# A two-layer convolution and attention kernel: pairing of products, column halves in attention, and other PSUM banks

## The chip, the cores and the metric

The kernel runs on one core of a Trainium2 chip. The metric is the device time of one execution in microseconds. Each engine (PE, the matrix engine; DVE, the vector engine; ACT, the scalar engine; POOL; and SP, which here only issues DMAs) works through its own queue in order, and they wait for one another by semaphores.

## The reference

The input is an image x of 384 channels and 192 × 192 pixels, float32. Two layers are applied, each as x + layer(group norm of x), with 32 groups of 12 channels:

```
layer 0:  qkv = W_qkv · x + b            # 384 -> 1152 channels per pixel
          qkv = 2x2 max pool of qkv      # 96 x 96 pixels
          qkv = depthwise 3x3 conv of qkv + b_dw
          q, k, v: 8 heads of 48 channels; q and k normed over the 9216 pixels
          attn = q · kᵀ * temperature    # 48 x 48 per head, over the pixels
          out = sum over 4 values of kk of  a_kk * softmax(top kk of attn) · v
          out = gelu(out), each pixel repeated 2x2, W_proj · out + b_proj
layer 1:  sign(x), shifted along the row by -3..3 by channel, times sign(W) (384 x 384), + bias
```

The attention weights per head are 48 × 48, so that layer 0 is mostly products over pixels: the qkv projection in float32 is by far the largest.

## The kernel before

The image is cut into 24 units (`NU`) of 8 rows; 384 channels are 3 tiles (`CT`) of 128 partitions. The stages are:

1. Statistics of x for the first group norm, while x streams through (ends at about 140 us).
2. q and k, for each of the 24 units and for m = 0 to 5 (3 tiles of q, 3 of k): `qkv_unit` makes three blocks of 512 pixels with 3 products each (L354) into the PSUM ring `qkv` of 3 banks; DVE takes the 2 × 2 maximum from PSUM (L364); ACT adds the bias (L373) and makes the first of the nine taps of the depthwise convolution (L380); DVE adds the other eight (L382); ACT keeps the last two rows for the next unit (L384). Below, a *tile* of work is such a run of `qkv_unit` for one unit and one m. A product in float32 appears in the profile as two matmul records with two weight loads; so a tile is 18 records of 512 columns. The result is transposed in 32 × 32 blocks (L410) and moved by 16 SP DMAs for each of q and k (L423, L428) into `room`, an SBUF buffer that holds one unit of q and k. `products` (L433 to L449) multiplies q and k of one unit into three PSUM banks `gram`, by halves of 64 columns (6 products for each 128 pixels); it is called for unit u − 1 after tile m = 2 of unit u (L465), and its instructions are pinned in program order. `gathered` (L470) does the last unit.
3. v, 24 units of 3 tiles, by the same `qkv_unit`, into `chunk` buffers in SBUF. In the first units the softmax steps (`softmaxes`, a generator, one step per tile) lie between the tiles. At its end it transposes the 384 × 384 weight matrix `full` into `aT` in 9 pieces, each a PE transpose into the one bank `p3ps` (L576) and an ACT copy (L577). After that, `attention(g)` (L626) treats 512 pixels: the array is used as four row tiles of 32 partitions, one for each pair of heads (p = 0 to 3); each multiplies its 32 rows of three channel tiles t, which are 96 channels of two heads, into 96 output columns and its own bank `ops`. Six GELUs on ACT (L644) take a block from PSUM back into `chunk`. There are 18 blocks (`NAB`); 16 are done between tiles of v, and two (`HOLD`) after the last tile, in an order written by hand.
4. Projection (L589, then the addition by DVE, L601) and layer 1: ACT takes the signs (L782), POOL shifts them, PE multiplies in fp8 (L801) into three double banks `l1ps`, DVE adds (L810), and DMAs store. For i = 0 to 3 the projections are ahead of the first layer-1 products; the projections use two banks `yps`.

Where nothing is pinned, a scheduler puts each engine's instructions in order; `manual_schedule` and `keep_in_program_order` fix the order as written. `pool.tile(name=...)` takes the next buffer of a ring of `bufs` and so waits for the users of the buffer that stood there.

How the channels of a head pair lie in a row tile matters for the change (`pair_rows`, L109): t = 0 holds 32 channels of the first head, t = 1 holds 32 of the second, and t = 2 holds the remaining 16 of each.

Of the kernel before, what the change touches and what calls it, by code (L numbers as in the profile page):

```python
# [10 lines left out]
F32 = mybir.dt.float32  # L11
# [4 lines left out]
AF = mybir.ActivationFunctionType  # L16
# [4 lines left out]
P = 128  # L21
# [128 lines left out]
def conv_preact_kernel(ctx: ExitStack, tc: tile.TileContext, a: dict, out: bass.AP):  # L150
# [192 lines left out]

        return (1 if u else 2), (PR if u < NU - 1 else PR + 1)

    def qkv_unit(pqkv, xt, u, m, pl, parts, before=None):


        x4 = xt.rearrange("p t (r w) -> p t r w", w=W)
        lo, hi = rows(u)  # L350
        for r0, nr, c0, ncol in BLOCKS:
            ps = pqkv.tile([P, 512], F32, name="qkv")
            for t in range(CT):
                ins = nc.tensor.matmul(  # L354
                    ps,
                    wq[:, t, m * P : (m + 1) * P],
                    x4[:, t, r0 : r0 + nr, c0 : c0 + ncol],
                    start=(t == 0),
                    stop=(t == CT - 1),
                )  # L360
                if m == CT and t == r0 == c0 == 0:

                    tc.keep_in_program_order(ins)
            nc.vector.tensor_reduce(  # L364
                pl[:, 2 + r0 // 2 : 2 + (r0 + nr) // 2, 1 + c0 // 2 : 1 + (c0 + ncol) // 2],
                ps.rearrange("p (i a j b) -> p i j a b", a=2, b=2, j=ncol // 2),
                AX.XY,
                ALU.max,
            )
        if before:  # L370
            before(pqkv.tile([P, 512], F32, name="qkv")[:, :NM])
        new = pl[:, 2 : 2 + PR, 1 : 1 + WP]
        nc.scalar.activation(new, new, AF.Identity, bias=bq[:, m : m + 1])  # L373
        for acc, r0, n in parts:
            acc2 = acc.rearrange("p (r w) -> p r w", w=WP)
            for k in range(9):
                r = lo - 1 + r0 + k // 3
                src = pl[:, r : r + n, k % 3 : k % 3 + WP]
                if k == 0:
                    nc.scalar.activation(acc2, src, AF.Identity, bias=bdw[:, m : m + 1], scale=wdw[:, m, 0:1])  # L380
                else:
                    nc.vector.scalar_tensor_tensor(acc2, src, wdw[:, m, k : k + 1], acc2, ALU.mult, ALU.add)  # L382
        if u < NU - 1:
            nc.scalar.copy(pl[:, 0:2, :], pl[:, PR : PR + 2, :])  # L384


    last_products = products_of_x.enter_context(ExitStack())
    pg = last_products.enter_context(tc.tile_pool(name="p2g", bufs=1, space=PSUM))
    with pairs, tc.tile_pool(name="p2t", bufs=2, side="right") as tp:
        gram = [pg.tile([P, 512], F32, name=f"gram{t}") for t in range(CT)]  # L390
        qkT = room[:, : 2 * size].rearrange("p (s n) -> p s n", s=2)

        def of_unit(u):

            lo, hi = rows(u)
            n = hi - lo + 1
            nk = -(-n * WP // P)
            q, k = qkT[:, 0, : nk * C], qkT[:, 1, : nk * C]
            return (
                n,  # L400
                nk,
                q.rearrange("p (t k c) -> p t k c", t=CT, k=nk),
                k.rearrange("p (b k c) -> p b k c", k=nk, c=B),
            )
# [46 lines left out]
        for u in range(NU):  # L451

            for v in range(u, u + KEEP + 1):
                if v not in kept:
                    kept[v] = unit(v % NU)
            xt = kept.pop(u)
            lo, hi = rows(u)
            n = hi - lo + 1
            for m in range(2 * CT):
                acc = tp.tile([P, (PR + 1) * WP], F32, name="dw")[:, : n * WP]  # L460
                qkv_unit(pqkv, xt, u, m, padded_qk[m], [(acc, 0, n)], None if u or m else bias)
                transposed(u, *divmod(m, CT), acc)
                sq = tp.tile([P, (PR + 1) * WP], BF16, name="sq", bufs=1)
                nc.scalar.activation(sq[:, : n * WP], acc, AF.Square, accum_out=ssq[:, m, u : u + 1])  # L464
                if u and m == CT - 1:  # L465
                    products(u - 1)
                if m % CT == CT - 1:
                    moved(u, m // CT)

# [8 lines left out]

    wpr = ctx.enter_context(tc.tile_pool(name="wpr", bufs=1)).tile([P, CT, C], F32, name="wpr")

    def softmaxes(p3, psp):


        ones = p3.tile([P, P], F32, name="ones")
# [78 lines left out]
        for t in range(CT):  # L563
            for j in range(DN[t] // HD):
                pair, second = divmod(HEAD0[t] + j, 2)
                for d, e0, e1 in (
# [3 lines left out]
                    nc.vector.tensor_scalar_mul(  # L570
                        full[:, t, d : d + e1 - e0], wsum[:, t, e0:e1], headm[:, t, j : j + 1]
                    )
        for t in range(CT):
            for k in range(CT):
                ps = psp.tile([P, P], F32, name="p3ps")
                nc.tensor.transpose(ps, full[:, t, k * P : (k + 1) * P], ident)  # L576
                nc.scalar.copy(aT[:, k, t * P : (t + 1) * P], ps)  # L577


    end = ctx.enter_context(ExitStack())  # L580
# [29 lines left out]
    with ExitStack() as vs:  # L610
# [5 lines left out]
        pool = first_pooled  # L616
        for t in pool:
            nc.gpsimd.memset(t[:, 0:2, :], 0.0)  # L618
        done, steps = 0, None

        def weights(name):
            wl = wp.tile([P, CT, C], F32, name="wl")
# [2 lines left out]

        def attention(g):  # L626

            c, b = divmod(g, CPX // ABLK)
            cols = slice(b * ABLK, (b + 1) * ABLK)
            pss = [po.tile([P, ABLK], F32, name="ops") for _ in range(NP)]  # L630
            for t in range(CT):
                for p in range(NP):
                    rows = slice(p * Q, (p + 1) * Q)
                    nc.tensor.matmul(  # L634
                        pss[p][:PAIR],
                        aT[rows, t, p * PAIR : (p + 1) * PAIR],
                        chunk[c][rows, t, cols],
                        start=(t == 0),
                        stop=(t == CT - 1),
                    )  # L640
            for p, ps in enumerate(pss):
                for t in [p] if p < CT else range(CT):
                    src, to = (slice(0, PAIR),) * 2 if p < CT else (slice(t * Q, (t + 1) * Q), slice(PAIR, P))
                    nc.scalar.activation(chunk[c][to, t, cols], ps[src], AF.Gelu, accum_out=osum[to, t, g : g + 1])  # L644

        for u in range(NU):
            xt = kept.pop(NU + u) if NU + u in kept else unit(u)
# [8 lines left out]
            for m in range(CT):  # L656
                parts = []
                for c in range(first // CR, last // CR + 1):
# [1 line left out]
                    parts.append(  # L660
                        (chunk[c][:, m, (r0 - c * CR) * WP : (r1 + 1 - c * CR) * WP], r0 - first, r1 + 1 - r0)
                    )
                qkv_unit(pqkv, xt, u, 2 * CT + m, pool[m], parts)
                if m == 0 and u == UC:

                    wl = weights("w_projG").rearrange("p t (g c) -> p t g c", c=GRP)
# [12 lines left out]
                    group_sums(bg, bpr.unsqueeze(2))  # L679
                    nc.vector.tensor_scalar_mul(bg1, bg, -1.0 / GRP)  # L680
                if u >= TOPK and steps is None:
                    steps = softmaxes(p3, psp)
                if steps:
                    if next(steps, 1):
                        steps = ()
                        scratch.close()
                        early = opened("p5x0", 1)
                elif steps == () and done < NAB - HOLD and (done + 1) * ABLK <= first * WP:
                    attention(done)
                    done += 1  # L690
        kept[FIRST[1] - 1] = unit(FIRST[1] - 1)
        with tc.manual_schedule():

            assert done == NAB - HOLD
            for g in range(done, NAB - 1):
                attention(g)
            for m in range(CT):
                projected(pqkv.tile([P, 512], F32, name="qkv")[:, :PPX], FIRST[0], m)
            attention(NAB - 1)

            projected(pqkv.tile([P, 512], F32, name="qkv")[:, :PPX], FIRST[1], 0)
            nc.vector.tensor_reduce(om, osum, AX.X, ALU.add)
            ys = [pqkv.tile([P, 512], F32, name="qkv")[:, :PPX] for m in range(1, CT)]
            projection(ys[0], FIRST[1], 1)
            projection(ys[1], FIRST[1], 2, range(1))
            ps = psp.tile([P, P], F32, name="p3ps")[:NG, :1]
            for t in range(CT):
                nc.tensor.matmul(ps, wg1[:, t], om[:, t : t + 1], start=(t == 0), stop=(t == CT - 1))
            nc.vector.tensor_scalar(gm, ps, -1.0 / (GRP * NPX), bg1, ALU.mult, ALU.add)
            projection(ys[1], FIRST[1], 2, range(1, 2))  # L710
            ps = psp.tile([P, P], F32, name="p3ps")[:, :CT].unsqueeze(2)
            spread(ps, gm)
            projection(ys[1], FIRST[1], 2, range(2, CT))
            added(ys[0], FIRST[1], 1, 0)
            nc.vector.tensor_add(nmean1, nmean0, ps[:, :, 0])
            added(ys[0], FIRST[1], 1, 1)
            for r in range(2):
                added(ys[1], FIRST[1], 2, r)
# [4 lines left out]
    with end:  # L723
# [18 lines left out]
        def summed(i, m):  # L742

            u = order[i]
            if i >= len(FIRST):
                projected(pyp.tile([P, PPX], F32, name="yps"), u, m)
            if m < CT - 1:
                return
            left[u // UC] -= 1
# [43 lines left out]
        def finished(i, m):  # L793
# [3 lines left out]
            for r0 in range(0, UR, 4):  # L797
                ps = psp.tile([P, 2, 512], F32, name="l1ps")
                for j in range(2):
                    for t in range(CT):  # L800
# [4 lines left out]
                            start=(t == 0),  # L805
                            stop=(t == CT - 1),
                        )
                px = slice(r0 * W, (r0 + 4) * W)
                blk = xt[:, m, px].rearrange("p (j n) -> p j n", j=2)
                nc.vector.scalar_tensor_tensor(  # L810
                    blk, ps[:, :, : 2 * W], bl1[:, m : m + 1], blk, ALU.add, ALU.add
                )
                if (i, m) == (NU - 1, CT - 1):
                    nc.sync.dma_start(ov[u, :, m, px], xt[:, m, px])
            if i + 3 >= NU and (i, m) != (NU - 1, CT - 1):
                nc.sync.dma_start(ov[u, :, m], xt[:, m])

# [104 lines left out]
```

## Time and profile before

Three timed runs took 2224.49, 2224.65 and 2229.05 us (median 2224.65). The profiled execution has a span of 2225.2 us at a granted TensorE clock of 0.998; its own time was 2227.01 us.

| engine | busy us | share of the span |
|---|---|---|
| PE | 2072.8 | 93% |
| DVE | 1902.6 | 85% |
| ACT | 819.6 | 37% |
| POOL | 211.3 | 9% |

| group | count | busy us | mean ns |
|---|---|---|---|
| L354 qkv matmul | 3888 | 1681.4 | 593 |
| L441 gram matmul (96 and 128 columns) | 876 | 90.7 | 248, 277 |
| L634 attention matmul | 432 | 52.0 | 601 |
| L644 GELU, 32 and 96 partitions | 108 | 63.1 | 587 |
| L382 depthwise taps, q and k | 1152 | 708.6 | 615 |
| L364 maximum | 648 | 441.5 | 682 |

Busy times of matmuls overlap one another since they are pipelined; what a run of them costs is read from the distance of their starts. In the chain of waits each line names the instruction that held up what came after it, with the time that it so accounts for; in the timeline the bracket at the end of a line is the idle time of the engine before it and what ended that.

### The profile page before, as it was taken

The numbers are of one execution on the slowest core, as the hardware profiler recorded it, in microseconds if no ns is written. First come the engines' busy times: TensorE is split into PE (matmuls) and PEld (weight loads), VectorE is DVE, ScalarE is ACT, GpSimd is POOL, SyncE is SP. The second block draws the span as 40 slices with busy tenths as digits, with TensorE's granted clock in tenths as the row PEclk, the third lists the DMA queues.
The fourth block names the chain that finished last, engine by engine and source line by source line (L and its number), as shares of the span: only waits on it lengthen the run. The fifth ranks groups of instructions, "written<-read, shape, count | busy, mean of one in ns | idle before, by whom it ended". The sixth has DMA issues, their size and how long they took to land.

```text
span 2225.2 us, 20427 instructions
## 1 busy us (share of the span) xinstructions
PE 2072.8 (93%) x6573; PEld 966.5 (43%) x6573; DVE 1902.6 (85%) x3270; ACT 819.6 (37%) x1419; POOL 211.3 (9%) x330
## 2 busy tenths in 40 slices
PE   0049999999999999999999999999999999999998
PEld 0024444444444444444444444443444444455555
DVE  5678888888888888888888899986787887899998
ACT  4542222222222222222222222225323233388886
POOL 1000000000000000000000000000000000177765
PEclk9999999999999999999999999999999999999999
DMA  9962222222222232222223213014221312379997
GB/s 398 417 280 64 64 69 71 84 87 72 67 64 71 68 103 71 72 64 66 72 70 101 70 33 121 28 49 175 85 85 45 125 43 86 128 295 407 424 425 319
DMA packets 209723, 302.73 MB, mean 136 GB/s; under 512 B 162224, under 2 KB 165072, under 8 KB 209616
## 3 DMA queue, kind: packets, MB, share of 16 engines
q1 hardware_dynamic: 199296, 248.18, 32.1%
q10 hardware_dynamic: 10320, 53.25, 5.8%
q8 instruction: 52, 0.85, 0.1%
q14 instruction: 55, 0.45, 0.1%
HBM read 216.04 MB, written 56.62 MB: 123 GB/s over the span
## 4 chain that ended last, share of the span: by engine, by line
PE 81%; DVE 11%; DMA 5%; ACT 1%; SPq 1%; issue 0%; DVEq 0%; ACTq 0%
PE qkv L354 64%; PE l1ps L801 6%; PE yps L589 6%; DVE chunk L382 5%; DMA xt<-in_x_dram 5%; DVE pooled L364 2%; PE gram L441 2%; PE ops L634 2%; DVE dw L382 1%; SPq L186 1%; DVE xt L601 1%; ACT chunk L380 0%; ACT pooled L373 0%; PE qkv L273 0%; SPq L428 0%
## 5 line engine op out<-in xcount | busy, mean ns | idle before, releaser
L354 PE MATMUL qkv<-xt,wq 128*128 128x512 f32 x3888 | 1681.4, 593 | 0.0
L354 PEld LDWEIGHTS qkv<-xt,wq 128*128 128x128 f32 x3888 | 734.4, 190 | 920.8 <-issue 837.1
L382 DVE SCALAR_TENSOR_TENSOR dw<-pooled,small,dw 128x384 f32<-128x384 f32 (+2 forms) x1152 | 708.6, 615 | 132.3 <-ACT dw L380 107.7
L364 DVE TENSOR_REDUCE pooled<-qkv 128x128 f32<-128x512 f32 x648 | 441.5, 682 | 37.9 <-PE qkv L354 37.3
L382 DVE SCALAR_TENSOR_TENSOR chunk<-pooled,small,chunk 128x384 f32<-128x384 f32 (+3 forms) x696 | 369.6, 545 | 71.4 <-ACT chunk L380 54.1
L384 ACT COPY pooled<-pooled 128x196 f32<-128x196 f32 x207 | 73.6, 356 | 756.6 <-DVE dw L382 536.8
L373 ACT ACTIVATE pooled<-pooled,small 128x384 f32<-128x384 f32 x216 | 133.0, 616 | 384.0 <-DVE pooled L364 373.5
L782 ACT ACTIVATE signs<-xt,nmean 64x1536 fp8e4<-64x1536 f32 x144 | 226.5, 1573 | 44.7 <-PE yps L589 26.0
L801 PE MATMUL l1ps<-signs,wb 128*128 128x384 fp8e4 x864 | 152.2, 326 | 0.0
L589 PE MATMUL yps<-chunk,wpr 128*128 128x384 f32 x396 | 141.2, 495 | 2.7 <-DVE xt L601 2.7
L601 DVE SCALAR_TENSOR_TENSOR xt<-yps,small,xt 128x768 f32<-128x768 f32 x132 | 128.1, 1012 | 13.8 <-PE yps L589 7.3
L273 PE MATMUL qkv<-wq,late 128*32 128x384 f32 x18 | 8.3, 622 | 140.3 <-ACT late L295 140.3
L810 DVE SCALAR_TENSOR_TENSOR xt<-l1ps,small,xt 128x768 f32<-128x768 f32 x144 | 138.3, 1007 | 0.0
L301 DVE BATCH_NORM_STATS2 room<-xt 128x6 f32<-128x512 f32 x144 | 88.1, 678 | 51.0 <-DMA xt<-in_x_dram 50.9
L618 POOL MEMSET pooled<- 128x196 f32 x3 | 0.8, 263 | 1285.6 <-DVE dw L382 1285.6
L464 ACT ACTIVATE sq<-dw 128x384 bf16<-128x384 f32 (+2 forms) x144 | 75.3, 523 | 120.7 <-DVE dw L382 120.6
L801 PEld LDWEIGHTS <-wb 128*128 128x128 fp8e4 x864 | 83.7, 97 | 72.3 <-issue 14.2
L380 ACT ACTIVATE dw<-pooled,small 128x384 f32<-128x384 f32 (+2 forms) x144 | 100.5, 698 | 2.2
L290 ACT ACTIVATE room<-xt 128x1536 bf16<-128x1536 f32 x48 | 71.2, 1483 | 66.4 <-DMA xt<-in_x_dram 65.7
L589 PEld LDWEIGHTS yps<-chunk,wpr 128*128 128x128 f32 x396 | 74.7, 193 | 45.8 <-issue 5.9
L410 DVE STREAM_TRANSPOSE blocks<-dw 128x384 f32<-128x384 f32 (+1 forms) x144 | 82.2, 571 | 4.2
L760 POOL COPY rest<-signs 9x384 int32<-9x384 int32 (+1 forms) x144 | 72.4, 503 | 67.3 <-ACT signs L782 61.9
(116 smaller groups left out, 576.9 us busy)
## 6 DMA issues: line engine op xcount, KB each, us to landing
xt<-in_x_dram SPq DMA_DIRECT2D x81, 2304.0 KB, 13.6
out_dram<-xt ACTq DMA_DIRECT2D x17, 2304.0 KB, 15.6
room<-blocks SPq DMA_DIRECT2D x736, 36.0 KB, 2.0
xt<-in_x_dram SPq DMA_DIRECT2D x26, 768.0 KB, 8.8
out_dram<-xt ACTq DMA_DIRECT2D x12, 768.0 KB, 8.6
out_dram<-xt SPq DMA_DIRECT2D x8, 768.0 KB, 4.8
wq<-in_w_qkvT_dram ACTq DMA_DIRECT2D x1, 1728.0 KB, 15.2
room<-blocks SPq DMA_DIRECT2D x32, 48.0 KB, 2.0
```

The costliest lines, as they stand in the source:

```text
L301: nc.vector.bn_stats(stats[b][:, t, at : at + 6], xt[:, t, j * 512 : (j + 1) * 512])
L354: ins = nc.tensor.matmul(ps, wq[:, t, m * P : (m + 1) * P], x4[:, t, r0 : r0 + nr, c0 : c0 + ncol], start=(t == 0), stop=(t == CT - 1),)
L364: nc.vector.tensor_reduce(pl[:, 2 + r0 // 2 : 2 + (r0 + nr) // 2, 1 + c0 // 2 : 1 + (c0 + ncol) // 2], ps.rearrange("p (i a j b) -> p i j ...
L373: nc.scalar.activation(new, new, AF.Identity, bias=bq[:, m : m + 1])
L380: nc.scalar.activation(acc2, src, AF.Identity, bias=bdw[:, m : m + 1], scale=wdw[:, m, 0:1])
L382: nc.vector.scalar_tensor_tensor(acc2, src, wdw[:, m, k : k + 1], acc2, ALU.mult, ALU.add)
L410: nc.vector.transpose(to[:, :full], acc[:, : full * P].rearrange("p (k j c) -> p k j c", j=NBP, c=B))
L589: nc.tensor.matmul(ps, wpr[:, t, m * P : (m + 1) * P], o[:, t, :], start=(t == 0), stop=(t == CT - 1),)
L601: nc.vector.scalar_tensor_tensor(x5[:, m, r], yb, bpr[:, m : m + 1], x5[:, m, r], ALU.add, ALU.add)
L782: nc.scalar.activation(rows_of(sg, p, SAT[t] - HSHIFT[t][h]), xt[p, t, :].rearrange("p (r w) -> p r w", w=W), AF.Sign, bias=nmean1[p, t : ...
L801: nc.tensor.matmul(ps[:, j, : 2 * W], wb[:, t, m * P : (m + 1) * P], rows_of(sg, slice(0, P), SAT[t])[:, r0 + 2 * j : r0 + 2 * j + 2], sta ...
L810: nc.vector.scalar_tensor_tensor(blk, ps[:, :, : 2 * W], bl1[:, m : m + 1], blk, ALU.add, ALU.add)
```

## The change

- q and k: `room` now holds two units. `products` of two units run one after the other, in even units (for u − 2 and u − 1), and once more in the last unit for the one left over. The last unit uses the buffer's first part and more.
- The bias products at the start write to the bank `gram0` instead of a bank of the `qkv` ring.
- The 9 transposes go, three by three, into three `ops` banks with one ACT copy of 384 columns for each.
- In the 16 attention blocks between tiles of v, each row tile's 96 output columns are made in two halves of 64 columns that overlap by 32: half 0 (columns 0 to 63, PSUM partitions 0 to 63) sums t = 0 and t = 2, half 1 (columns 32 to 95, partitions 64 to 127) sums t = 1 and t = 2. So there are 2 steps of 8 products instead of 3 steps of 4. The GELUs of a block become 13, in pieces of 16, 32 and 48 partitions. The last two blocks are made as before, with the fourth bank's GELUs first.
- `attention` becomes a generator: its GELUs are issued at a new point (`amid`) in the next two tiles of v, between the taps and the copy of the two rows, and pinned there; a new block starts only when the one before has ended, so at most every third tile.
- For i = 2 and 3 of layer 1 the projection of m = 2 writes to an `l1ps` bank instead of `yps`.
- In the last tile of layer 1 each addition of 768 columns becomes two of 384, each with its own store, on the SP and the ACT queue in turn.

```diff
-            before(pqkv.tile([P, 512], F32, name="qkv")[:, :NM])
+            before()
...
-                qkv_unit(pqkv, xt, u, m, padded_qk[m], [(acc, 0, n)], None if u or m else bias)
+                qkv_unit(pqkv, xt, u, m, padded_qk[m], [(acc, 0, n)], None if u or m else lambda: bias(gram[0][:, :NM]))
...
+        result = amid()
         if u < NU - 1:
             nc.scalar.copy(pl[:, 0:2, :], pl[:, PR : PR + 2, :])
+        return result
...
-            q, k = qkT[:, 0, : nk * C], qkT[:, 1, : nk * C]
+            at = 0 if u == NU - 1 else u % 2 * CT * UPX // 2
+            q, k = (room[:, at + s * nk * C : at + (s + 1) * nk * C] for s in range(2))
...
-                if u and m == CT - 1:
-                    products(u - 1)
+                if m == CT - 1 and u and (u % 2 == 0 or u == NU - 1):
+                    for v in range(max(u - 2, 0) if u % 2 == 0 else u - 1, u):
+                        products(v)
...
-        for t in range(CT):
-            for k in range(CT):
-                ps = psp.tile([P, P], F32, name="p3ps")
-                nc.tensor.transpose(ps, full[:, t, k * P : (k + 1) * P], ident)
-                nc.scalar.copy(aT[:, k, t * P : (t + 1) * P], ps)
+        for k in range(CT):
+            ps = po.tile([P, ABLK], F32, name="ops")[:, :C]
+            for t in range(CT):
+                nc.tensor.transpose(ps[:, t * P : (t + 1) * P], full[:, t, k * P : (k + 1) * P], ident)
+            nc.scalar.copy(aT[:, k], ps)
...
+            split = g < NAB - HOLD
+            sides = ((0, 0), (PAIR - HALF, HALF)) if split else ((0, 0),)
+            n = HALF if split else PAIR
+            for i in range(2 if split else CT):
+                for h, (o, at) in enumerate(sides):
+                    t = (h, CT - 1)[i] if split else i
+                    for p in range(NP):
+                        rows = slice(p * Q, (p + 1) * Q)
+                        nc.tensor.matmul(
+                            pss[p][at : at + n],
+                            aT[rows, t, p * PAIR + o : p * PAIR + o + n],
+                            chunk[c][rows, t, cols],
+                            start=(i == 0),
+                            stop=(t == CT - 1),
+                        )
+            for p in (NP - 1, *range(NP - 1)):
+                ps = pss[p]
+                if p in (NP - 1, 1):
+                    yield
+                if split:
+                    moves = ((HALF, Q, Q), (0, 0, HD), (HALF + Q, 2 * Q, Q))
+                else:
+                    moves = ((0, 0, PAIR),)
...
+                        if split:
+                            tc.keep_in_program_order(ins)
+            yield
...
-                elif steps == () and done < NAB - HOLD and (done + 1) * ABLK <= first * WP:
-                    attention(done)
-                    done += 1
+                elif steps == ():
+                    if not block and done < NAB - HOLD and (done + 1) * ABLK <= first * WP:
+                        block = attention(done)
+                        next(block)
+                        done += 1
...
-                projected(pyp.tile([P, PPX], F32, name="yps"), u, m)
+                if i < 4 and m == CT - 1:
+                    ps = psp.tile([P, 2, 512], F32, name="l1ps")[:, 0, :PPX]
+                else:
+                    ps = pyp.tile([P, PPX], F32, name="yps")
+                projected(ps, u, m)
...
+                last = (i, m) == (NU - 1, CT - 1)
+                for js in (range(1), range(1, 2)) if last else (range(2),):
...
+                    if last:
+                        (nc.scalar if js[0] else nc.sync).dma_start(ov[u, :, m, px], xt[:, m, px])
```

## The prediction

> **What bounds the kernel now.** I began with the chain of waits on the page, which says what holds the end, and then asked for the same chain in pieces, which says stage by stage what the PE time consists of. From the page:
>
> ```profile
> PE 81%; DVE 11%; DMA 5%; ACT 1%; SPq 1%; issue 0%; DVEq 0%; ACTq 0%
> ```
>
> The 11% of DVE is nearly all between 1273 and 1510 us. In the PE timeline of 1361 to 1486 us, however, 290 qkv matmuls stand in 124.62 us, 0.430 us each, the rate of the stages where PE alone is named: there both engines are full, and less DVE work would not help. So from 149 to 1923 us what counts is how long PE's own queue takes. The chain by pieces (start, length, what), first in the q/k stage, then in the v stage:
>
> ```profile
> 270.40 1.80 PE gram L441 x36
> 272.19 46.55 PE qkv L354 x108
> 318.74 1.79 PE gram L441 x36
> ```
>
> ```profile
> 1510.59 7.92 PE qkv L354 x18
> 1518.51 2.76 PE ops L634 x24
> ...
> 1553.32 23.37 PE qkv L354 x54
> 1576.69 2.76 PE ops L634 x24
> ...
> 1605.59 46.55 PE qkv L354 x108
> ```
>
> Three run lengths give the price of a matmul and of a visit. From 18 to 54 records: (23.37 − 7.92)/36 = 0.429 us per 512-column record. A run of 54 is thus 23.17 us of matmul and 0.20 us of something paid once per run; 2 × 23.37 − 46.55 = 0.19 says the same. Each time PE leaves qkv for other work and comes back, qkv's side loses 0.19 us.
>
> What a visit does inside is in the timeline of weight loads and matmuls (start, length, engine, line, what, how many):
>
> ```profile
> 1518.44 0.26 PEld L634 LDWEIGHTS ops<-chunk,aT 32*96 32x96 f32 x8 [0.76 <-issue]
> 1518.44 2.83 PE L634 MATMUL ops<-chunk,aT 32*96 32x512 f32 x24
> ...
> 1518.95 0.18 PEld L634 LDWEIGHTS ops<-chunk,aT 32*96 32x96 f32 x4 [0.25 <-issue]
> ...
> 1519.38 0.18 PEld L634 LDWEIGHTS ops<-chunk,aT 32*96 32x96 f32 x4 [0.25 <-issue]
> ```
>
> The reader should see waves: two sets of four weights first, then four more every 0.43 us. Four row tiles work at once; 24 records are 6 waves, 6 × 0.429 = 2.58 us, and 0.18 us are fill and drain.
>
> **What the Trainium skill says.** "TensorEngine Tiling (Array Packing)", section Tiling Modes, lists a 32×64 configuration with 8 independent tiles, and says that a change of mode drains the engine. The drain agrees with the 0.19 + 0.18 us above; eight tiles at once no record of before shows, only its two halves: 4 row tiles (ops) and 2 column tiles (gram). The same page, Restrictions and Gotchas, says that different row tiles cannot use one PSUM bank at the same time; the changed loop keeps one bank per row tile p and puts the column halves on different partitions of it. "TensorE: Matmul & The Clock Gate", Part 1, says that an idle PE falls to half clock; the windows of 1944 to 1950 us agree with a granted clock of 0.50.
>
> **The attention, 16 of 18 blocks.** 12 products of 96 columns in 3 steps become 16 products of 64 columns in 2 steps, 32 records. If 8 tiles run at once these are 4 waves: 4 × 0.429 + 0.18 = 1.90 us against 2.76, or 0.86 less per block; 16 × 0.86 = 13.7 us, all on PE's path. Other end: the two column halves take turns, 8 waves, 3.62 us, 0.86 more per block. Issue is no obstacle that I can see: 32 records in 1.72 us are 54 ns each, and gram's 36 in 1.79 us are 50. Gram also shows two column tiles with different moving data truly overlapping: per k tile each half has 96 + 96 + 128 = 320 columns, over 3 k tiles and 2 records at 0.429/512 that is 1.61 us, while in series it would be 3.2. I take 4 waves.
>
> **Products of two units together.** Visits in the q/k stage fall from 24 to 13 (11 pairs, one single, the last). Each of the 11 saved visits gives back qkv's 0.19 and gram's own fill, 1.79 − 1.61 = 0.18, of which I count 0.15 since some is per record and stays: 11 × 0.34 = 3.7 us. Ends: 2.1 (qkv's side alone) and 4.1. The q/k DMAs are the same in number and queue; slots now alternate, and the writer of a slot waits for products issued just before it, as it does now. The k transfer ahead of the last products stays.
>
> **Transposes.** 9 products that alternate with qkv through one bank become 9 in a row into three banks, with 3 copies in place of 9:
>
> ```profile
> 1485.78 0.27 PE L576 MATMUL p3ps<-ident,full 128*128 128x128 f32 x1
> 1485.88 1.02 PE L354 MATMUL qkv<-xt,wq 128*128 128x512 f32 x2
> ...
> 1488.76 0.33 PE L576 MATMUL p3ps<-ident,full 128*128 128x128 f32 x1 [0.88 <-ACT aT L577]
> ```
>
> From 1485.78 to the first ops at 1495.81 are 10.03 us, of which 18 qkv records are 7.73; 2.3 remain. Each transpose delays the next by 0.10 to 0.11, so 9 in a row are 1.0. Gain 1.3 us (0.9 to 1.5). The copies have the next qkv tile, 7.7 us, to land in before attention reads aT.
>
> **GELUs.** 6 activations per block become 13 (the partitions of a half no longer lie in one piece), 7 × 0.73 us = 5.1 us more ACT per block, 82 us in all (0.59 us for one, and with the accumulator read the 32-partition ones of the block at 1609 us follow one another by 0.69 to 0.81). They are pinned between L380 of the next two tiles and L384, 7 in the first, 6 in the second. Behind them on ACT wait L384, then L373 of the tile after, and DVE's taps wait for that. Today L373 starts about 6.1 us after L380 has ended (1597.66 to 1603.81); 7 × 0.73 + 0.36 for L384 are 5.5. The next block's ops need the banks back 7.7 us after a qkv tile; L373, L380 and 6 GELUs end about 7.0 us after it. Both fit, by 0.6 to 0.7 us. I put the cost at 0.
>
> **Bias, last tile, third bank.** The bias products keep their 2.10 us and only leave the qkv ring; right after them the chain has one unbroken run of 144 qkv records: 0. In the last tile two additions of 1.0 us become four. A 768-column addition holds DVE for 0.97 us, a 384-column one for about 0.6, so the end of DVE moves by up to +0.4; the last transfer is 192 instead of 384 KB, and with queues at 414 GB/s in 2215 to 2220 us, that is 0.47 us less. I take 0 (−0.5 to +0.4). At the start of the last stage, DVE waits for PE, which waits for the two yps buffers:
>
> ```profile
> 1951.55 3.88 DVE L601 SCALAR_TENSOR_TENSOR xt<-yps,small,xt 128x768 f32<-128x768 f32 x4 [0.92 <-PE yps L589]
> 1955.85 3.88 DVE L601 SCALAR_TENSOR_TENSOR xt<-yps,small,xt 128x768 f32<-128x768 f32 x4 [0.42 <-PE yps L589]
> 1960.15 1.94 DVE L601 SCALAR_TENSOR_TENSOR xt<-yps,small,xt 128x768 f32<-128x768 f32 x2 [0.43 <-PE yps L589]
> ```
>
> With m = 2 in another bank the waits of 0.42 and 0.43 go: 0.8 us (0 to 1.5). The 0.92 and the half clock before it stay.
>
> **Sum.** 13.7 + 3.7 + 1.3 + 0.8 = 19.5 us off the span of 2225.2, that is 2205.7. The timed runs have their median at 2224.65, 0.55 below this span, so I predict 2205.1.
>
> **Rivals.**
>
> Column halves take turns (slower). Place: the 16 ops visits; price: 8 waves, +13.7 in place of −13.7, while the rest still gives 5.8: 2232.6. It decides once a visit costs over 2.76 + 5.8/16 = 3.12 us, which is from seven waves on. For it: no 32×64 record in the trace. Against: both halves of the mode overlap already, gram with two moving streams at once. 8%.
>
> ACT's GELUs become the wait. The groups between 1508 and 1892 us (busy, mean, then idle time before and its releasers):
>
> ```profile
> L382 DVE SCALAR_TENSOR_TENSOR chunk<-pooled,small,chunk 128x384 f32<-128x384 f32 (+2 forms) x438 | 227.5, 535 | 54.0 <-ACT chunk L380 39.5 <-ACT pooled L373 6.2
> L364 DVE TENSOR_REDUCE pooled<-qkv 128x128 f32<-128x512 f32 x131 | 89.2, 684 | 26.3 <-PE qkv L354 25.8
> ```
>
> DVE's real slack is the 26 us in which it waits for PE. This stretch has 354/24 = 14.75 blocks and so loses 12.7 us; 13 are left over 44 tiles, 0.3 us each. Two tiles in three carry GELUs, so a delay of 0.46 us per such tile is free, one of 0.7 us costs 32 × 0.24 = 8 us: 2213. For it: margins of only 0.6 us, and banks held for two tiles. Against: ACT is busy for 137 of 384 us now. 13%.
>
> Visits are cheaper to merge than thought, or gain nothing (records cost more when eight tiles load weights, gram's drain stays): 5 waves instead of 4, 6.9 us less gain, 2212. 5%.
>
> No change to speak of, the pieces cancelling: 2%. Forecast: 72%, with its own range 2202 to 2209.
>
> **Range and chances.** The forecast's part up and down, with the two rivals of 2212 to 2213 taken in, gives 2200 to 2214; the taking of turns is left out. A change of over 0.2%, 4.4 us, can be told from none: faster 0.90, same 0.02, slower 0.08.
>
> **What would show it.** Ops visits of about 1.9 us with eight weights per 0.43 us; qkv runs of 216 records with gram visits of 72 records near 3.4 us; the transposes in about 1 us; in the v stage runs of 54 still 23.37 us long. Wrong: ops of 3 us or more; qkv runs longer than 23.4 with "ACT" as releaser on DVE, or ops waiting for "ACT chunk".

## The result, and the profile after

The changed kernel takes 2213.81 us (median of 4 runs, 2213.45 to 2214.3) against 2225.99 us (4 runs) for the kernel before: a ratio of 0.9944, with a 95% interval of 0.9926 to 0.9961. The prediction was 2205.1 us, with 2200 to 2214 us as its range and faster as its likeliest case. So the kernel became faster, by about 12 us where 19.5 were forecast. The profiled spans are 2211.8 and 2225.2 us; the 13.4 us between them are what is explained below.

Both traces were cut at the same points of the program. Each row gives the moment at which its point is passed, and what the stage since the point above gained.

| point in the program | before, us | after, us | gained in the stage | forecast |
|---|---|---|---|---|
| first qkv record | 149.44 | 149.41 | 0.0 | 0 |
| PE back to qkv after the last gram visit | 1337.72 | 1333.87 | 3.8 | 3.7 |
| first ops record | 1495.81 | 1490.72 | 1.2 | 1.3 |
| first record of block 16 | 1922.93 | 1914.09 | 3.8 | 13.7 |
| addition that makes nmean1 | 1941.38 | 1932.77 | −0.2 | 0 |
| first layer-1 product | 1959.95 | 1945.60 | 5.7 | 0.8 |
| end | 2225.2 | 2211.8 | −0.9 | 0 |

The rows of q and k's products and of the transposes are as forecast. The attention stage gave 10 us less than forecast, and the start of layer 1 gave 5 us more.

The chain by engine, from the page of the kernel after, shows the shift that has to be explained: ACT's share went from 1% to 4% and DVE's from 11% to 13%.

```profile
PE 75%; DVE 13%; DMA 5%; ACT 4%; SPq 1%; issue 1%; POOL 0%; DVEq 0%; ACTq 0%
```

In the q/k stage the chain by pieces of the kernel after has the forecast visits:

```profile
271.82 92.90 PE qkv L354 x216
364.72 3.44 PE gram L443 x72
```

Two units with their visit now take 96.34 us, where one took 48.34 before (from the start of one gram visit to the next, 270.40 to 318.74 us): a merged visit saves 0.35 us. The visits of attention, in the timeline of PE and its weight loads after, are as forecast too:

```profile
1490.72 0.23 PEld L648 LDWEIGHTS ops<-chunk,aT 32*64 32x64 f32 x16 [0.76 <-ACT chunk L380]
1490.72 1.97 PE L648 MATMUL ops<-chunk,aT 32*64 32x512 f32 x32
1491.20 0.18 PEld L648 LDWEIGHTS ops<-chunk,aT 32*64 32x64 f32 x8 [0.25 <-issue]
1491.63 0.18 PEld L648 LDWEIGHTS ops<-chunk,aT 32*64 32x64 f32 x8 [0.25 <-issue]
```

Two sets of eight weights at first, then eight every 0.43 us: eight tiles work at once, and 32 records are four waves. But the chain by pieces of the attention stage after shows that the visits' gain was not kept everywhere:

```profile
1544.92 23.37 PE qkv L354 x54
1568.29 1.90 PE ops L648 x32
1570.19 7.94 PE qkv L354 x18
...
1621.98 1.96 PE ops L648 x26
1623.94 23.37 PE qkv L354 x54
1647.31 1.90 PE ops L648 x32
```

Where PE is not held up, 25.27 us lie between the starts of two blocks (23.37 and 1.90). Between 1578 and 1622 us PE falls off the chain, and DVE and ACT stand in its place (left out above). The intervals between the starts of blocks 0 to 15 are 26.3, 26.0, 25.3, 25.3, **26.5, 27.2**, 25.3, 25.3, **26.5, 27.2**, 25.3, 25.3, **26.5, 27.2** and 25.3 us. The long pairs lie at the borders of `chunk`, every fourth unit, where each tile of v has its taps in two parts and ACT has six first taps (L380) in a unit in place of three. One such border in the timeline of the kernel after:

```profile
1595.63 8.10 DVE L382 SCALAR_TENSOR_TENSOR chunk<-pooled,small,chunk 128x96 f32<-128x96 f32 x17
...
1604.39 15.72 PE L354 MATMUL qkv<-xt,wq 128*128 128x512 f32 x36 [1.00 <-DVE pooled L364]
...
1616.76 0.59 ACT L671 ACTIVATE chunk<-ops 32x512 f32<-32x512 f32 x1
...
1617.60 0.59 ACT L671 ACTIVATE chunk<-ops 48x512 f32<-48x512 f32 x1
...
1620.04 1.08 PE L648 MATMUL ops<-chunk,aT 32*64 32x512 f32 x6
...
1620.07 0.36 ACT L385 COPY pooled<-pooled 128x196 f32<-128x196 f32 x1
1620.43 0.59 ACT L671 ACTIVATE chunk<-ops 48x512 f32<-48x512 f32 x1
1621.13 0.59 ACT L671 ACTIVATE chunk<-ops 32x512 f32<-32x512 f32 x1
1621.98 0.24 PEld L648 LDWEIGHTS ops<-chunk,aT 32*64 32x64 f32 x16 [1.75 <-ACT chunk L671]
1621.98 1.96 PE L648 MATMUL ops<-chunk,aT 32*64 32x512 f32 x26 [0.86 <-ACT chunk L671]
```

There are two different waits here. First DVE does 17 taps in a row, no maximum (L364) between them; the qkv ring is not emptied, and PE waits 1.00 us. Then the visit of block 5 begins at 1620.04, can do six records only, and waits for the GELUs of block 4 that still hold the other banks.

### The profile page after: what moved, and what is told of

Read it like the earlier page. It is cut to its first block, busy times and chain, and to the rows that moved or that the text cites. A ratio compares the mean times of both kernels' runs of the same rounds, so it can differ in the third digit from the quotient of the medians.

```text
span 2211.8 us, 20840 instructions
## 1 busy us (share of the span) xinstructions
PE 2055.5 (93%) x6701; PEld 960.5 (43%) x6701; DVE 1906.0 (86%) x3272; ACT 909.1 (41%) x1637; POOL 211.2 (10%) x330
## 4 chain that ended last, share of the span: by engine, by line
PE 75%; DVE 13%; DMA 5%; ACT 4%; SPq 1%; issue 1%; POOL 0%; DVEq 0%; ACTq 0%
PE qkv L354 60%; DVE chunk L382 7%; PE l1ps L844 6%; PE yps L593 5%; DMA xt<-in_x_dram 5%; DVE pooled L364 3%; ACT chunk L671 2%; PE gram L443 2%; DVE dw L382 1%; PE ops L648 1%; ACT chunk L380 1%; SPq L186 1%; ACT pooled L373 1%; DVE xt L605 1%; PE qkv L273 0%
## 5 line engine op out<-in xcount | busy, mean ns | idle before, releaser
L364 DVE TENSOR_REDUCE pooled<-qkv 128x128 f32<-128x512 f32 x648 | 441.3, 683 | 64.4 <-PE qkv L354 64.1
L385 ACT COPY pooled<-pooled 128x196 f32<-128x196 f32 x207 | 73.6, 356 | 664.0 <-DVE dw L382 543.6
L373 ACT ACTIVATE pooled<-pooled,small 128x384 f32<-128x384 f32 x216 | 133.0, 616 | 421.9 <-DVE pooled L364 408.6
L856 DVE SCALAR_TENSOR_TENSOR xt<-l1ps,small,xt 128x768 f32<-128x768 f32 (+1 forms) x146 | 138.6, 997 | 0.0
L593 PE MATMUL yps<-chunk,wpr 128*128 128x384 f32 x384 | 134.2, 486 | 0.3 <-DVE xt L605 0.3
L671 ACT ACTIVATE chunk<-ops 32x512 f32<-32x512 f32 (+3 forms) x220 | 129.7, 589 | 8.7 <-PE ops L648 4.4
L380 ACT ACTIVATE dw<-pooled,small 128x384 f32<-128x384 f32 (+2 forms) x144 | 100.1, 695 | 1.5
```

Source lines behind the costliest of these rows:

```text
L364: nc.vector.tensor_reduce(pl[:, 2 + r0 // 2 : 2 + (r0 + nr) // 2, 1 + c0 // 2 : 1 + (c0 + ncol) // 2], ps.rearrange("p (i a j b) -> p i j ...
L593: nc.tensor.matmul(ps, wpr[:, t, m * P : (m + 1) * P], o[:, t, :], start=(t == 0), stop=(t == CT - 1),)
L671: ins = nc.scalar.activation(chunk[c][to : to + k, t, cols], ps[at + j : at + j + k], AF.Gelu, accum_out=osum[to : to + k, t, g : g + 1],)
L856: nc.vector.scalar_tensor_tensor(blk, ps[:, js[0] : js[-1] + 1, : 2 * W], bl1[:, m : m + 1], blk, ALU.add, ALU.add)
```

## Experiments

Each kernel below is the kernel before or the kernel after with one edit. Where no number of runs is given, the kernel ran once; what is compared are mainly the same stretches of the profiles. "The stage" is the time from the first ops record to the first of block 16: 427.1 us before, 423.4 after. Without any wait it would be 412.1 after (15 intervals of 25.27 and a last one of 33.0); before, 1.3 us of its 427.1 are a wait at the second block, which the forecast's 13.7 us (the products alone) did not count. So the kernel after loses 11.3 us in this stage to waits.

**1. GELUs at once** (kernel after)

```diff
-                        if split:
-                            tc.keep_in_program_order(ins)
...
-                elif steps == ():
-                    if not block and done < NAB - HOLD and (done + 1) * ABLK <= first * WP:
-                        block = attention(done)
-                        next(block)
-                        done += 1
+                elif steps == () and done < NAB - HOLD and (done + 1) * ABLK <= first * WP:
+                    list(attention(done))
+                    done += 1
```

> The changed kernel with its attention blocks issued as before: a new one after any tile, its 13 GELUs right behind it, not pinned to later tiles. Column halves and all other parts stay. Measure: time from the first ops matmul to the first of block 16 (427.1 us before, 423.4 after; 413.4 if all 16 visits gave back 0.86 us). Theory A, the GELUs moved to later tiles hold the ops banks and the ACT queue too long: about 414 us. Theory B, 13 GELUs instead of 6 are too much for ACT wherever they stand: 13 x 0.70 = 9.1 us then stand in one tile in front of L373, and the stage is no shorter than 423 us. Theory C, the order of DVE's taps, in which 17 taps in a row follow from a block every third tile: that order is gone here (the longest run is 14 past the first blocks), so about 414 us if the GELUs do no harm.

Measured: 2287.83 us, and 494.2 us for the stage. This is far beyond what any of the theories said. The waits from 1500 to 1980 us (engine, line, waited for: us in total, times, longest):

```profile
DVE chunk L382 <- ACT chunk L380: 100.5, 35, 8.5
...
PEld ops L648 <- DVE chunk L382: 29.1, 10, 4.9
```

From 1601 us in this kernel 13 GELUs stand in a row, until L373 can start at 1611.07 us; DVE's waits for a first tap (L380) reach 8.5 us at a time. PE's clock suffers as well: in nine stretches of the stage, 44 us together, the trace has it at 0.50 of full speed, where the kernel after has none. Theory A in its simple form falls: the kernel with 13 GELUs made at once loses far more than that with 13 pinned into later tiles. This edit also changes where the blocks are put, so how much each of these takes is open.

**2. Whole columns, GELUs late** (kernel after)

```diff
-            split = g < NAB - HOLD
+            split = False
+            late = g < NAB - HOLD
...
-                        if split:
+                        if late:
                             tc.keep_in_program_order(ins)
```

> The changed kernel with whole 96-column products (3 steps, 6 GELUs) in all blocks, but a block at most every third tile and its GELUs pinned in the next two tiles, as changed. Visits cost 2.76 us again, so without waits the stage from first ops to block 16 takes 427.1 us less the 1.3 that the kernel before waits at its second block: 425.8. Theory A (banks held) and C (17 taps in a row, which stay in this order): waits of some us in each of three stretches stay, 428 us or more. Theory B (13 GELUs): with 6 no waits, 426 us.

Measured: 2216.16 us; the stage 426.0 us, all its intervals 26.13 us but the first (26.28). Hardly a wait is left (0.2 us in all), though blocks stand at every third tile, banks are held for two tiles and DVE has its 17 taps in a row. With 6 GELUs, and the visit of 2.76 us, all that is harmless, as theory B says.

**3 and 4. The number of GELUs and the length of the visit, crossed.** The first has column halves with 6 GELUs; it leaves out the GELUs that bring the columns of both halves to the right rows, so some rows hold other values. The second has whole columns, taken out of PSUM in 13 pieces.

```diff
-                    moves = ((HALF, Q, Q), (0, 0, HD), (HALF + Q, 2 * Q, Q))
+                    moves = ((0, 0, PAIR),)
```

```diff
# on top of experiment 2
-                    moves = ((0, 0, PAIR),)
+                    moves = ((Q, Q, Q), (0, 0, HD), (2 * Q, 2 * Q, Q)) if late else ((0, 0, PAIR),)
```

> The changed kernel with its column halves (visits of 1.90 us), but only 6 GELUs per late block, with the partitions of whole columns; the GELUs that put the right columns of the two halves into place are left out, so the values in those rows are other ones. Measure as before: first ops matmul to block 16 (423.4 us in the changed kernel, 426.0 with whole columns and 6 GELUs). Theory B, the number of GELUs on ACT: without waits, 25.27 us from block to block all through and 412 to 414 us in all. Theory D, DVE (its taps and maxima, 26 us per unit at the chunk borders, whatever ACT does) is the limit once a visit is below 2.76 us: intervals of 26.5 and 27.2 us stay at three borders and the stage stays at 420 us or more.

> Whole columns (visits of 2.76 us) with 13 GELUs per late block, in the same pieces of 16, 32 and 48 partitions as in the changed kernel. Theory B: 26.13 us from block to block where nothing waits, but again longer intervals at the chunk borders, the sum above 426.0, about 428 to 431. Theory D: 426.0 as with 6 GELUs.

The stage in the four kernels, in us:

| | 6 GELUs | 13 GELUs | the 7 more cost |
|---|---|---|---|
| whole columns, visit 2.76 | 426.0 | 433.6 | 7.6 |
| column halves, visit 1.90 | 415.6 | 423.4 | 7.8 |
| the halves give | 10.4 | 10.2 | |

Within 0.2 us the two edits add up: neither changes what the other costs. The kernel with halves and 6 GELUs takes 2206.18 us in all. Of the 11.3 us of waits, 7.8 are the seven more GELUs. In the same stretch of this kernel, the visit of block 5 is whole:

```profile
1619.10 1.90 PE ops L648 x32
1621.00 23.37 PE qkv L354 x54
```

The other 3.5 us (1.0 in the first interval, 0.8 at each border) stay with 6 GELUs: that is theory D's part. There PE waits for DVE's maxima behind the 17 taps, 0.56 us at the first border:

```profile
1603.38 15.72 PE L354 MATMUL qkv<-xt,wq 128*128 128x512 f32 x36 [0.56 <-DVE pooled L364]
```

With whole columns and 6 GELUs only 0.2 us of waits remain. As I read it, the longer visit gives DVE the time: with halves the interval at a border is 26.10 us, and with whole columns every interval is 26.13 us.

**5. Halves in half of the blocks** (kernel after; whole columns in blocks 0, 1, 4, 5, 8, 9, 12, 13)

```diff
-            split = g < NAB - HOLD
+            split = g < NAB - HOLD and g % 4 > 1
+            late = g < NAB - HOLD
...
-                        if split:
+                        if late:
                             tc.keep_in_program_order(ins)
```

> The changed kernel with whole columns and 6 GELUs in blocks 0, 1, 4, 5, 8, 9, 12 and 13, those after which the changed kernel waits (26.0 to 27.2 us to the next block), and column halves in the other eight. Theory B: all intervals after whole blocks 26.13, after the others 25.27; the stage 4 us shorter than in the changed kernel, 419 us, and the whole 2209 to 2210 us. Theory D: the shorter visits just ahead of a border still meet DVE's limit, so the stage is 421 us or more and the whole within 2 us of the changed kernel, 2212 to 2214.

Measured: 2209.61 us (4 runs), 0.9923 of the kernel before (0.9906 to 0.994). The whole is as theory B said, the stage, 420.3 us where 419 were expected, not quite: the 27.2 became 26.13, but the 26.5 before them stayed. So the second of each pair goes with the GELUs (experiment 11 tests of which block). The first is for the larger part DVE's: with 6 GELUs in every block (experiment 3) it is 26.1, 0.8 us above 25.27, and the other 0.4 goes with the seven more GELUs.

**6 and 7. Another tile of the unit without GELUs** (kernel after, blocks one or two tiles of v later)

```diff
                 elif steps == ():
-                    if not block and done < NAB - HOLD and (done + 1) * ABLK <= first * WP:
+                    slot += 1
+                    if slot >= 1 and not block and done < NAB - HOLD and (done + 1) * ABLK <= first * WP:
```

(for the second, `slot >= 2`; slot starts at −1)

> The changed kernel with its 16 blocks all one tile of v later, so that another tile of each unit (the second after the one before) is the one without GELUs; DVE's order then has runs of 19 taps in place of 17 at the chunk borders. If the waits come from GELUs meeting the tiles at a border where ACT has six L380 in place of three, the waits change with the tile: stage from first ops to block 16 between 414 and 432 us, less the 7.7 us by which the first block is later than in the changed kernel; two long intervals at each border in place of 26.54 and 27.20. If only the number of GELUs in a period counts, whatever the tile, the excess over 25.27 per border stays at 3.2 us.

> As the last, two tiles later; here DVE has runs of 17 taps and of 14 at every border. If the place of the GELUs counts, the excess over 25.27 us per border differs from 3.2 us; if only their number does, it stays at 3.2.

Measured: 2211.1 and 2217.86 us. The excess over 25.27 us per border is 1.6 and 1.8 us in place of 3.2, in one interval (26.88 and 27.04) in place of two. So the place counts, not only the number. One tile later DVE has runs of 19 taps at the borders, yet PE waits there only for ACT's GELUs. (Of the 2211.1 us, 1.7 are lost elsewhere, see experiment 11.) Two tiles later block 15 meets the end of the stage: block 16 waits 4.26 us for ACT's GELUs, PE then runs at a granted clock of 0.50 from 1914.3 to 1921.1 us, and nmean1 is made at 1937.23 us, 4.5 us later than in the kernel after. That costs more than the borders give.

**8. Bias alone** (kernel before)

```diff
-            before(pqkv.tile([P, 512], F32, name="qkv")[:, :NM])
+            before()
...
-                qkv_unit(pqkv, xt, u, m, padded_qk[m], [(acc, 0, n)], None if u or m else bias)
+                qkv_unit(pqkv, xt, u, m, padded_qk[m], [(acc, 0, n)], None if u or m else lambda: bias(gram[0][:, :NM]))
```

> The kernel before with one edit, the bias products go to the gram bank instead of a bank of the qkv ring. Theory R, the ring then stands one bank further for the whole program, so that the first yps bank of the last stage is one that DVE has emptied long before: the first yps product no longer waits for DVE (2.3 us before), PE keeps its full clock, and the first l1ps product starts 3 to 5 us sooner after the nmean1 addition than before (18.6 us before, 12.8 after). Theory S, the third bank for m = 2 did that: no change here, 18.6 us.

Measured: 2222.53 us; 13.69 us from nmean1 to the first layer-1 product, 4.9 less than before. The start of the last stage in this kernel, and then in the kernel before (timeline, PE and DVE):

```profile
1941.23 0.91 PE L589 MATMUL qkv<-chunk,wpr 128*128 128x384 f32 x2
1941.41 2.86 DVE L601 SCALAR_TENSOR_TENSOR xt<-qkv,small,xt 128x768 f32<-128x768 f32 x3
1941.98 2.10 PE L589 MATMUL yps<-chunk,wpr 128*128 128x384 f32 x6
```

```profile
1941.28 0.91 PE L589 MATMUL qkv<-chunk,wpr 128*128 128x384 f32 x2
1944.47 8.97 PE L589 MATMUL yps<-chunk,wpr 128*128 128x384 f32 x18 [2.28 <-DVE xt L601]
```

An edit almost 1800 us earlier removed the wait. The ring of three `qkv` banks is dealt out in turn; with one bank fewer taken at the start, each later user has another bank. Before, the first `yps` bank would be the one that DVE read last, and now it is not: the trace names no banks, but here yps starts while DVE still reads qkv banks, and before it waited for that. Theory R holds. With the wait also goes PE's half clock after it: before, the granted clock is 0.50 from 1943.6 to 1950.4 us and the first 12 yps records take 7.05 us in the chain; here the clock is full from 1930 to 1960 us, and the first 6 stand in 2.10 us.

**9. Third bank alone** (kernel before)

```diff
-                projected(pyp.tile([P, PPX], F32, name="yps"), u, m)
+                if i < 4 and m == CT - 1:
+                    ps = psp.tile([P, 2, 512], F32, name="l1ps")[:, 0, :PPX]
+                else:
+                    ps = pyp.tile([P, PPX], F32, name="yps")
+                projected(ps, u, m)
```

> The kernel before with one edit, the projection of m = 2 for i = 2 and 3 in an l1ps bank. Theory R: the first yps product still waits for DVE and runs at half clock; only the waits of 0.4 us between DVE and PE go, first l1ps product about 17.8 us after the nmean1 addition (18.6 before). Theory S: most of the 5.8 us gained there by the whole change: about 13 to 14 us.

Measured: 2226.02 us; 16.31 us from nmean1 to the first layer-1 product, 2.3 less than before, with the first yps product still waiting 2.28 us. Theory R had 0.8 here (17.8 us). The rest fits the half clock after the wait, which lasts 3.4 us here and 6.8 in the kernel before: half of the difference is 1.7 us. Why it is shorter is open. Where the half clock is gone already, the third bank is worth 0.9 (13.69 us in experiment 8, 12.83 in the kernel after, which has both), the forecast's 0.8.

**10. Last tile whole** (kernel after)

```diff
-                last = (i, m) == (NU - 1, CT - 1)
+                last = False
...
-                    if last:
-                        (nc.scalar if js[0] else nc.sync).dma_start(ov[u, :, m, px], xt[:, m, px])
+                    if (i, m) == (NU - 1, CT - 1):
+                        nc.sync.dma_start(ov[u, :, m, px], xt[:, m, px])
```

> The changed kernel with the last tile's additions and stores in one piece each, as before. Theory: from the end of PE's last matmul to the end of the span it takes 7.8 us as in the kernel before, against 7.4 in the changed one; the split is worth 0.4 us. Rival: DVE's four pieces cost what the smaller last transfer gives, 7.4 us here too.

Measured: 2213.63 us. From the end of PE in the chain to the end of the span it is 8.21 us here, 8.34 in the kernel after, and 7.79 before. (The expectation set 7.8 and 7.4 side by side, read from two different views; the chain's ends are the ones to compare.) The same stretch is 8.22 us in experiment 8, without the split, and 7.32 in experiment 5, with it: it varies by more than the split could give, and no gain shows, as its rival said.

**11. Whole columns in every fourth block** (kernel after; blocks 0, 4, 8 and 12 whole)

```diff
-            split = g < NAB - HOLD
+            split = g < NAB - HOLD and g % 4 > 0
+            late = g < NAB - HOLD
...
-                        if split:
+                        if late:
                             tc.keep_in_program_order(ins)
```

> The changed kernel with whole columns and 6 GELUs in blocks 0, 4, 8 and 12 only. In the changed kernel the long interval after block 5 (27.20 us) is the visit of block 5 waiting for banks that the 13 GELUs of block 4 still hold; the one after block 4 (26.54) is DVE's 17 taps in a row, which here absorb the longer visit. Theory B with this reading: the intervals after blocks 1, 5, 9 and 13 fall to 25.27, those after 0, 4, 8 and 12 stay at 26.2 to 26.6; the stage from first ops to block 16 is 423.4 - 0.7 - 3 x 1.93 = 416.9 us, and the whole 2206 to 2207 us, below the kernel with halves in half the blocks (2209.6). If instead the wait of block 5 comes from its own 13 GELUs or from DVE alone, 27.2 stays and the whole is 2213 us or more.

Measured: 2207.98 us (5 runs, 2207.16 to 2208.87), 0.9915 of the kernel before (0.9901 to 0.9928): better than both kernels. The stage is 416.9 us, the intervals 26.3, 25.3, 25.3, 25.3, 26.5, 25.3 and so on, as forecast. The chain at the border:

```profile
1605.38 15.72 PE qkv L354 x36
1621.10 1.90 PE ops L649 x32
1623.01 23.37 PE qkv L354 x54
```

Block 5 no longer waits, since block 4 has 6 GELUs; and block 4's longer visit costs nothing, since DVE's wait was there to take it. The whole missed the 2206 to 2207 us by 1 us. In the profiled execution the first 252 qkv records after the bias took 110.04 us, where the kernel after has 108.35 for the same records: the granted clock is 0.50 from 160.3 to 163.7 us here (and likewise in the first kernel of experiments 6 and 7), and full in the kernel after.

## Why the prediction was right or wrong

**Direction: right. Range: right with luck.** The likeliest case was faster, and 2213.81 lies just inside the upper end of the range. Two errors of opposite sign brought it there. The attention stage gave 10.0 us less than forecast: 7.8 for the GELUs and 3.5 for DVE, less a wait of 1.3 us in the kernel before that was not counted. The start of layer 1 gave 4.9 us more, from a place that no case had; without it the kernel would have taken about 2218.7 us, outside the range. So the forecast of 2202 to 2209 did not come true, and the second rival (13%, 2213) had the right cause for the larger part of the loss, but met its total by the same luck.

**Products of two units: right.** 3.8 us against 3.7. The reading of the run lengths, 0.19 us on qkv's side and 0.15 inside the visit, was enough: a merged visit saved 0.35 us in place of 0.34.

**Transposes: right.** 1.2 us against 1.3; nine in a row take 1.0 us (1481.92 to the next qkv record at 1482.90).

**Eight tiles at once: right.** 1.90 us per visit was forecast and measured, so the rival on the slower side falls. The Trainium skill, "TensorEngine Tiling (Array Packing)", section Tiling Modes, lists 32×64 as eight independent tiles, and the trace agrees: eight matmuls in each 0.43 us.

**GELUs at a cost of 0: this step failed.** The prediction found that 7 GELUs and L384 (L385 in the kernel after) fit ahead of L373 by 0.6 us, and 6 fit before the next visit by 0.7. It worked this out for one ordinary tile, with 0.73 us from one GELU to the next. In the kernel after the pieces follow one another by 0.69 to 0.84 us, 0.78 on average, which takes about half of each margin. Where nothing else is added they still fit: the six ahead of block 4 end at 1593.35 us, 0.15 us before its visit. At a border of `chunk` two more things come in. ACT has further first taps of 96 columns (0.47 us each), and DVE's order puts 17 taps in a row there and lets L373 come late. Six GELUs, with L385 between, reach from 1616.76 to 1621.9 us, and the next visit, at 1620.04, finds its banks held. Experiments 2 to 4 show the size: 7.6 to 7.8 us for seven more GELUs per block, at either length of visit. The rival named the engine and the held banks, and 8 us as the price. It had this as 0.24 us in each of 32 tiles, however, and the runs show it in four places: 0.7 us at the second interval and 2.4 us at each of three borders (the kernel after against experiment 3). That the sums agree is chance.

**The visits' gain all on PE's path: this step was off too.** With 6 GELUs the halves give 10.4 us, not 13.7: 3.5 us go to waits for DVE in the first interval and at the borders, which the longer visits had covered (all but 0.2). The prediction counted DVE's slack as an average, 26 us in the stage; the borders had none.

**Bias for nothing: this step failed, to the good.** "The bias products keep their 2.10 us and only leave the qkv ring: 0" is right where the bias is made, but it overlooked what comes of leaving a ring. It is worth 4.9 us alone, at the far end of the program. The profile had the sign of it: the wait of 2.28 us ahead of the first yps product was in the trace, and the prediction took it, with the half clock, as something that stays.

**Third bank and last tile: right.** The third bank gave 0.9 us against 0.8, and the last tile no gain against 0. The last stage itself became 0.9 us longer. Of that, 0.56 us lie behind the end of PE, where the runs vary by more than that (experiment 10). The other 0.4 come before: from the first layer-1 product to the end of PE it is 257.5 us in the kernel before, 257.5 and 257.6 in experiments 8 and 9, and 257.9 in the kernel after. A wait of DVE for a load, 1.47 us at 1967 us, is new in the kernel after, but it is not the cause: experiment 10 has no such wait and the same 257.9 us. What the cause is, was not tested.

**A reading that is too broad.** Of DVE's 11% of the chain before, 8.5 points lie between 1273 and 1510 us, as the prediction says; the other 2 lie between 1888 and 1958 us, around block 16 and the first projections. No term of the sum rests on this.

## What to carry to other kernels

When a busy engine gets shorter work, ask what else used the time: take the slack of the other engines at the tightest place of the loop, not over the stage. Splitting a product's output to fill the array can multiply the instructions that empty PSUM (here from 6 to 13), and these can take back most of the gain (here 7.8 of 10.4 us); measure both edits crossed, since a mixture (here whole columns in every fourth block) can be better than either. And taking one buffer out of a ring moves every later user of it by one, so look at which waits in the trace depend on the turn.

## What was not expected of the hardware

A GELU with accumulator output takes about 0.59 us for 512 columns whether it covers 16, 32, 48 or 96 partitions. From its start to that of the next GELU it is 0.57 to 0.71 us for 96 partitions (0.62 on average, in the kernel before) and 0.69 to 0.84 for the pieces (0.78 on average, in the kernel after). So one GELU of 96 partitions, cut into three, costs nearly four times as much (3 × 0.78 against 0.62 us).

A wait of PE of 2.28 us, with a half clock after it, cost more by the clock than by the wait: in the kernel before 12 yps records took 7.05 us, where 3.9 us is their price at full clock (1.94 us for six, at 2187 us in its chain).
